# Three stages of a four-layer network kernel: the norm ahead of an involution in a hand-written order, a recurrence in runs of 32 tokens, an expert choice in three pieces

## The chip, the cores and the metric

The kernel runs on one core of a Trainium2 chip. The core has five engines that work side by side: TensorE (PE in the profile; PEld is its loading of weights), VectorE (DVE), ScalarE (ACT), GpSimd (POOL) and SyncE (SP), which in this kernel issues most of the DMAs. They meet through semaphores. SBUF is the memory on the core, 128 partitions wide, and PSUM is the memory that TensorE writes its results to, in eight banks of 512 floats for each partition. The metric is device time in microseconds for the whole program. Three runs of the kernel before gave a median of 8871.85 us (8869.74 to 8875.66).

## The reference

A tensor x of 4 batches, 128 channels and 64 by 64 positions passes four layers. Each has a mixer over positions and a feed-forward part over tokens, each behind a norm over the channels and with its input added back. Three of these eight parts are changed. Cut to what matters, they compute:

```python
def _ln_c(v, eps=1e-6):            # _ln_t is the same over the last axis
    m = jnp.mean(v, axis=1, keepdims=True)
    s = jnp.var(v, axis=1, keepdims=True)
    return (v - m) / jnp.sqrt(s + eps)

# layer 0, mixer: involution, 7 x 7 taps, dilation 2, 8 groups
red = jnp.einsum('bchw,oc->bohw', x, w_reduce) + b_reduce[None, :, None, None]   # 128 -> 32 channels
ker = jnp.einsum('bohw,ko->bkhw', red, w_span) + b_span[None, :, None, None]
...
out = jnp.einsum('bgckhw,bgkhw->bgchw', patches, ker)

# layer 0, feed-forward: a recurrence over the 4096 tokens of a batch
Wx = (flat - mean) * jax.lax.rsqrt(var + BN_EPS) * gamma + beta      # flat = x @ W.T, over all tokens
def step(yt, wx_t):
    yt = jax.nn.sigmoid(wx_t + yt @ Vt)
    return (yt, yt)

# layer 3, feed-forward: two of eight experts for each token
router_probs = jax.nn.softmax(x @ router_w + router_b, axis=-1)
top_p, top_i = jax.lax.top_k(router_probs, K)
top_p = top_p / jnp.sum(top_p, axis=-1, keepdims=True)
...
return jnp.einsum('bnk,bnkc->bnc', top_p, gathered)
```

## The kernel before

The activations stay in SBUF for the whole program, in a tile `xs` of 128 channels by 4 batches by 4096 tokens. Eight phases work on it one after another. A norm over channels is done with TensorE. A matmul with `cent` (the identity less 1/128) takes the mean off 512 tokens, a chunk. ScalarE squares the result, and matmuls with `ewin`, four of them in the four 32-column groups of the array, sum the squares of four chunks into rows of one bank. From that bank come one square root and one reciprocal. A matmul with `ident` then spreads a row of reciprocals over the partitions, and VectorE multiplies. The helper `centred` (L62) does this in two halves, with the square root between them.

A planner orders the instructions, engine by engine, by readiness and position in the program. Inside a block `tc.manual_schedule(engines=ORDERED)` the order of TensorE, ScalarE, VectorE and GpSimd is the order of the code; SyncE's isn't in `ORDERED`.

**Front of the involution (L228 to L279).** For each batch the centred half of the next batch and the scaling half of this one are issued, and the planner weaves them. The normed chunks land in the middle of padded row tiles, 76 wide, of which there are 16: eight for each of two batches in turn. L263 writes each row tile to `inv_image` in DRAM (304 KB). L268 reduces a chunk to 32 channels, repeated four times over the 128 partitions; L276 adds the bias, and L277 writes 256 KB to `inv_reds`. `load` (L211) reads back what a band of 16 rows needs, 16 shifted DMAs of 266 KB and one of 512 KB, all on SyncE's queue. The loads of the first two bands stand behind batches 2 and 3.

**Band loop (L337 to L361).** The pool of its tiles opens at L285. It takes the memory of the front's tiles, so L285 waits for their last use. Sixteen bands follow; band n+2 is loaded when band n is done, since the loaded tiles have two buffers.

**Recurrence (L364 on).** The norm of all 32 chunks (L382) is written to `xn`, laid out like `xs`. 32 matmuls with W and 32 `bn_stats` (L389, L390) give the statistics over all tokens, and these are folded into `wt` and `shift`. Then the 4096 tokens of a batch are cut into 64 runs of 64 tokens, and all runs step together. A first sweep of 20 steps from the run's end gives each run's last state, a second sweep of 64 steps starts each run from its neighbour's. The two pairs of batches, g = 0 and 1, alternate. A step is one matmul by `vt` on top of the inputs (L456) and one sigmoid (L461). The inputs of 4 steps at a time come from one matmul (L439), whose columns are read from `xn` with a step of 64 words. L467 adds the states to `xs`. Between the sweeps is a branch on `flag`, for weights whose row sums are beyond a bound; the branch's body isn't run here.

**Expert choice (L1590 on).** Four chunks make a quad, and a quad's eight halves are the loop of L1734. In a half, `gated` spreads gates over the partitions (L1718) and multiplies (L1724) for the half after it, TensorE multiplies by experts (L1742), and then one piece of `prepare` for the next quad is run by `next(side)`. One of these pieces was all of `choose` (L1637), some thirty small VectorE operations.

Of the kernel before, what the change touches and what calls it, by code (L numbers as in the profile page):

```python
# [17 lines left out]
F32 = mybir.dt.float32  # L18
BF16 = mybir.dt.bfloat16
I32 = mybir.dt.int32  # L20
# [8 lines left out]
P = 128  # L29
# [135 lines left out]


def as_shape(t, like):

    return t.rearrange("p (r w) -> p r w", w=W) if len(like.shape) == 3 else t
# [13 lines left out]
def involution(net):  # L183
# [17 lines left out]
    with ExitStack() as ctx:  # L201
        dram = ctx.enter_context(tc.tile_pool(name="inv_dram", bufs=1, space=bass.MemoryType.DRAM))
        image = dram.tile([B, P, SIDE * SIDE + EXTRA], F32, name="inv_image")
        reds = dram.tile([B, P, N], F32, name="inv_reds")
# [6 lines left out]
        def load(band):  # L211
# [4 lines left out]
            nc.sync.dma_start(red, reds[b, :, r * SPAN : (r + 1) * SPAN])  # L216
# [10 lines left out]
        with tc.tile_pool(name="inv_a", bufs=2) as sb, tc.tile_pool(name="inv_a_ps", bufs=2, space=PSUM) as ps:  # L227
            wred = sb.tile([P, TAPS, CR], F32, name="wred", bufs=1)  # L228
            bred = sb.tile([P, 1], F32, name="bred", bufs=1)
            for k in range(TAPS):  # L230
                nc.sync.dma_start(wred[:, k, :], ins["L0_conv_w_reduce"])
                nc.sync.dma_start(bred[k * CR : (k + 1) * CR], ins["L0_conv_b_reduce"])
            zero = sb.tile([P, PAD * SIDE + EXTRA], F32, name="inv_zero", bufs=1)
            nc.vector.memset(zero, 0.0)
            for b in range(B):
                nc.sync.dma_start(image[b, :, 0 : PAD * SIDE], zero[:, 0 : PAD * SIDE])
                nc.sync.dma_start(image[b, :, (PAD + H) * SIDE : SIDE * SIDE + EXTRA], zero)
            rows = [
                [sb.tile([P, ROWS, SIDE], F32, name=f"inv_rows{i}_{c}", bufs=1) for c in range(NCH)]
                for i in range(2)  # L240
            ]
            for i in range(2):
                for t in rows[i]:
                    nc.gpsimd.memset(t, 0.0)
# [7 lines left out]

            def inside(b, c):
                return rows[b % 2][c][:, :, PAD : PAD + W]

            second = net.centred([0], 1e-6, inside, sb, ps, 4, 2)
            for b in range(B):
                after = net.centred([b + 1], 1e-6, inside, sb, ps, 4, 2) if b + 1 < B else None
                second()
                second = after  # L260
                for c in range(NCH):
                    first = (PAD + c * ROWS) * SIDE
                    nc.sync.dma_start(  # L263
                        image[b, :, first : first + ROWS * SIDE],
                        rows[b % 2][c].rearrange("p r x -> p (r x)"),
                    )
                    pr = ps.tile([P, CH], F32, name="inv_pr", tag="pr")
                    nc.tensor.matmul(  # L268
                        as_shape(pr, inside(b, c)),
                        wred.rearrange("p k r -> p (k r)"),  # L270
                        inside(b, c),
                        start=True,
                        stop=True,
                    )
                    rd = sb.tile([P, CH], F32, name="inv_rd", tag="inv_rd")
                    nc.scalar.activation(rd, pr, AF.Identity, bias=bred)  # L276
                    nc.sync.dma_start(reds[b, :, c * CH : (c + 1) * CH], rd)  # L277
                if b >= B - 2:
                    loaded.append(load(b - (B - 2)))  # L279
# [84 lines left out]
def recurrence(net):  # L364

    tc, nc, ins = net.tc, net.nc, net.ins
    with (
# [13 lines left out]
        xn = sb.tile([P, B, N], F32, name="rnn_xn")  # L381
        net.layernorm(range(B), 1e-5, lambda b, c: xn[:, b, c * CH : (c + 1) * CH], sb, ps, 3)  # L382


        stats = sb.tile([P, B * NCH, nc.vector.BN_STATS_DIM], F32, name="rnn_stats")
        for j in range(B * NCH):
            b, c = divmod(j, NCH)
            pw = ps.tile([P, CH], F32, name="rnn_pw", tag="pd", bufs=3)
            nc.tensor.matmul(pw, wt, xn[:, b, c * CH : (c + 1) * CH], start=True, stop=True)  # L389
            nc.vector.bn_stats(stats[:, j, :], pw)  # L390
# [12 lines left out]
        nc.tensor.transpose(pt[:, 0:P], w, net.ident)  # L403
        nc.vector.tensor_copy(wt, pt[:, 0:P])

# [1429 lines left out]
```

## Time and profile before

The profiled execution took 8533.12 us, of which its span, from the first to the last instruction, is 8531.3 us. It is a single execution, and the median of the three timed runs is 338.7 us above it.

| What | us |
|---|---|
| Median of three runs | 8871.85 |
| Profiled execution | 8533.12 |
| Its span | 8531.3 |
| TensorE busy in the span | 7867.6 |
| VectorE busy | 5591.7 |
| GpSimd busy | 4943.6 |
| ScalarE busy | 3623.6 |

| Stage | from and to, us from the span's start |
|---|---|
| front of the involution, until L285 | 0 to 147.87 |
| bands of the involution | 151.82 to 1221.8 |
| norm and statistics of the recurrence | 1221.8 to 1339.4 |
| first sweep | 1342.4 to 1376.2 |
| second sweep | 1380.1 to 1488.8 |
| expert choice, steady part | 8098 to 8531 |

The page gives busy time by engine, and an engine can be busy in one stage and idle in another, so the stages are read one by one. Where an engine stood idle, the trace names what released it. A wait is put down to the last semaphore that came.

### The profile page before, as it was taken

The numbers are of one execution on the slowest core, as the hardware profiler recorded it, in microseconds if no ns is written. First come the engines' busy times: TensorE is split into PE (matmuls) and PEld (weight loads), VectorE is DVE, ScalarE is ACT, GpSimd is POOL, SyncE is SP. The second block draws the span as 40 slices with busy tenths as digits, with TensorE's granted clock in tenths as the row PEclk, the third lists the DMA queues.
The fourth block names the chain that finished last, engine by engine and source line by source line (L and its number), as shares of the span: only waits on it lengthen the run. The fifth ranks groups of instructions, "written<-read, shape, count | busy, mean of one in ns | idle before, by whom it ended". The sixth has DMA issues, their size and how long they took to land.

```text
span 8531.3 us, 146057 instructions
## 1 busy us (share of the span) xinstructions
PE 7867.6 (92%) x59834; PEld 3483.4 (41%) x59834; DVE 5591.7 (66%) x8297; ACT 3623.6 (42%) x6855; POOL 4943.6 (58%) x2479
## 2 busy tenths in 40 slices
PE   8999998677786688988999999999999999999899
PEld 2333324455555554443444344443444434444233
DVE  5777764688888843226676676776777667677155
ACT  2222222344444441040555555555555555555411
POOL 1444430477777710000888788887888878888600
PEclk8999998899999999997999999999999999999999
DMA  5333310688787723031455455454455544455400
GB/s 182 77 84 71 70 25 4 171 246 237 219 249 208 209 82 131 1 130 40 97 111 110 96 108 108 102 108 106 98 111 107 108 100 105 107 104 110 89 19 21
DMA packets 300201, 951.19 MB, mean 111 GB/s; under 512 B 41925, under 2 KB 114693, under 8 KB 241669
## 3 DMA queue, kind: packets, MB, share of 16 engines
q0 software_dynamic: 142848, 671.18, 33.4%
q1 hardware_dynamic: 156676, 270.60, 10.8%
q8 instruction: 472, 7.73, 0.4%
q14 instruction: 205, 1.67, 0.1%
HBM read 466.83 MB, written 72.17 MB: 63 GB/s over the span
## 4 chain that ended last, share of the span: by engine, by line
PE 55%; DVE 3%; issue 1%; DMA 1%; ACT 1%; POOL 0%; SPq 0%; DVEq 0%; ACTq 0%; POOLq 0%
PE att_pv L1444 15%; PE att_sc L1531 13%; PE att_mx L1388 10%; PE att_sc L1432 5%; PE conv_po L1198 3%; PE top_po L1742 3%; PE top_pw L1718 1%; DVE att_most L1399 1%; DMA moe_w<-in_L_ffn_weight 1%; PE att_sc L1361 0%; PE att_sc L1492 0%; PE att_sc L1475 0%; PE att_mx L1286 0%; PE att_sc L1322 0%; PE moe_acc L995 0%
## 5 line engine op out<-in xcount | busy, mean ns | idle before, releaser
L1463 POOL TENSOR_TENSOR att_acc<-att_acc,att_ex 128x2048 f32<-128x2048 f32 x640 | 2902.1, 4535 | 639.0 <-ACT att_ex L1532 619.7
L1399 DVE TENSOR_REDUCE att_most<-att_mx 128x2 f32<-128x1024 f32 x2016 | 2462.2, 1222 | 1071.7 <-PE att_mx L1388 990.8
L1532 ACT ACTIVATE att_ex<-att_sc 128x512 f32<-128x512 f32 x4096 | 2223.7, 594 | 1772.7 <-PE att_sc L1531 1488.1
L1531 PE MATMUL att_sc<-att_q,att_k 32*128 32x512 f32 x8192 | 2456.6, 606 | 0.0
L1388 PE MATMUL att_mx<-att_k,att_q 32*128 32x512 f32 x8064 | 2293.1, 647 | 12.9 <-DVE att_parts L1411 10.8
L1432 PE MATMUL att_sc<-att_rows,att_ones_b 32*128 32x256 bf16 (+1 forms) x6144 | 1502.6, 306 | 4.8 <-ACT att_ex L1532 4.7
L708 POOL DMA_INDIRECT dcn_g<-dcn_table,dcn_idx x1152 | 1100.0, 955 | 434.9 <-DMA dcn_g<-dcn_table,dcn_idx 119.9
L1444 PE MATMUL att_pv<-att_ex,att_vals 128*32 128x256 f32 x16384 | 1310.3, 391 | 0.0
L319 DVE SCALAR_TENSOR_TENSOR inv_prod<-inv_pk,bspan,inv_seen 128x1024 f32<-128x1024 f32 (+1 forms) x672 | 822.2, 1275 | 228.2 <-PE inv_pk L302 228.2
L1388 PEld LDWEIGHTS att_mx<-att_k,att_q 32*128 32x128 f32 x8064 | 611.1, 185 | 867.5 <-issue 707.2
L317 POOL TENSOR_TENSOR inv_prod<-inv_seen,inv_prod 128x1024 f32<-128x1024 f32 x224 | 528.4, 2359 | 679.1 <-ACT inv_prod L316 533.8
L1444 PEld LDWEIGHTS att_pv<-att_ex,att_vals 128*32 128x32 f32 x16384 | 322.6, 108 | 1319.7 <-issue 1301.5
L749 PE MATMUL dcn_pt<-ident,dcn_sum 128*128 128x128 f32 x2304 | 520.4, 310 | 336.3 <-DVE dcn_sum L733 335.9
L1531 PEld LDWEIGHTS att_sc<-att_q,att_k 32*128 32x128 f32 x8192 | 818.6, 183 | 11.0 <-issue 8.3
L722 ACT ACTIVATE dcn_one<-dcn_g,dcn_w 128x128 f32<-128x128 f32 x1152 | 456.3, 401 | 724.1 <-DMA dcn_g<-dcn_table,dcn_idx 719.2
L302 PE MATMUL inv_pk<-inv_red,wtap 32*96 32x512 f32 (+1 forms) x3584 | 605.7, 637 | 7.8 <-DMA inv_seen<-inv_image 7.8
L316 ACT ACTIVATE inv_prod<-inv_pk,bspan 128x1024 f32<-128x1024 f32 x224 | 249.2, 1113 | 820.9 <-PE inv_pk L302 811.8
L749 PEld LDWEIGHTS dcn_pt<-ident,dcn_sum 128*128 128x128 f32 x2304 | 374.7, 204 | 419.1 <-DVE dcn_sum L733 417.9
L333 PE MATMUL inv_out<-inv_prod,inv_fold 96*32 96x512 f32 (+1 forms) x3584 | 505.8, 606 | 18.3 <-DVE xs L355 18.3
L748 PE MATMUL dcn_pt<-ident,dcn_one 128*128 128x128 f32 x2304 | 477.4, 291 | 18.1 <-ACT dcn_one L722 18.1
L748 PEld LDWEIGHTS dcn_pt<-ident,dcn_one 128*128 128x128 f32 x2304 | 400.0, 205 | 228.3 <-issue 151.2
L725 DVE TENSOR_SCALAR dcn_part<-dcn_g,dcn_w 128x128 f32<-128x128 f32 x1152 | 405.6, 352 | 120.5 <-DMA dcn_g<-dcn_table,dcn_idx 87.7
(329 smaller groups left out, 7419.2 us busy)
## 6 DMA issues: line engine op xcount, KB each, us to landing
att_sum<-att_ex POOLq DMA_DIRECT2D x320, 1024.0 KB, 7.3
inv_seen<-inv_image SPq DMA_DIRECT2D x256, 266.0 KB
moe_w<-in_L_ffn_weight SPq DMA_DIRECT2D x64, 1024.0 KB
dcn_table<-dcn_xt SPq DMA_DIRECT2D x64, 512.0 KB
att_sum<-att_ex SPq DMA_DIRECT2D x32, 1024.0 KB
att_sum<-att_acc POOLq DMA_DIRECT2D x32, 1024.0 KB, 7.1
dcn_g<-dcn_table,dcn_idx POOLq DMA_INDIRECT x1152, 3.7
inv_image<-inv_rows SPq DMA_DIRECT2D x32, 304.0 KB
```

The costliest lines, as they stand in the source:

```text
L302: nc.tensor.matmul(pk[0:m, h, :], wtap[rg, unit, blk, 0:m], red[rg, h * CH : (h + 1) * CH], start=True, stop=True,)
L319: nc.vector.scalar_tensor_tensor(out=of, in0=pk[0:m].rearrange("p h (r x) -> p (h r) x", x=W), scalar=by, in1=view, op0=ALU.add, op1=ALU.mult,
L708: nc.gpsimd.indirect_dma_start(out=g, out_offset=None, in_=rows, in_offset=bass.IndirectOffsetOnAxis(ap=idx[:, j + i, k : k + 1], axis=0),)
L748: nc.tensor.matmul(out, one_, net.ident, start=i == 0, stop=False)
L749: nc.tensor.matmul(out, s, net.ident, start=False, stop=i == 3)
L1388: nc.tensor.matmul(pm[i] if alone else pm[:, i, :], q[r, t * P : (t + 1) * P], ks[r, kc * CH : (kc + 1) * CH], start=True, stop=True,)
L1399: nc.vector.tensor_reduce(most[:, 2 * half : 2 * half + 2, kc], pm, AX.X, ALU.max)
L1432: nc.tensor.matmul(pe[:, cols], ones_b[r], lows[g][r, cols], start=cols.start == 0, stop=False)
L1444: nc.tensor.matmul(block["pv"][r, cols], vals[b][:, t, r], ex[:, h, cols], start=t == 0 and half == 0, stop=t == NT - 1 and half == 1,)
L1463: nc.gpsimd.tensor_add(block["acc"], block["acc"], ex)
L1531: nc.tensor.matmul(pe, ks[r, t * P : (t + 1) * P], qs[c][r], start=False, stop=True)
L1532: nc.scalar.activation(ex[:, h, :], pe, AF.Exp)
```

## The change

There are three edits.

**The front of the involution.** `centred` is replaced by a new helper `normed_groups`, inside a manual order. It goes batch by batch, with the scaling of the batch before woven in after every fourth chunk; variances lag two chunks; the centred chunks go to tiles `ln_d` of their own, copied by ScalarE in batches 1 and 3 and by VectorE in batches 0 and 2. Products then go to 8 row tiles in a ring instead of 16. The reduction to 32 channels is no longer repeated. Four chunks go into the four column groups of one bank, so that there are 8 activations and 8 DMAs to `inv_reds` where there were 32 of each, and `load` reads its part with four DMAs of 32 partitions, one for each repetition. The loads of the first two bands are issued in batch 1.

```diff
+        for p in range(B // n):
+            pv, squares = bank("pv"), []
+            for j in range(PN):
+                stat(p, j, pv, squares)
+                if j % 4 == 1 and j > 4:
+                    variances(j // 4 - 1, pv, squares)
+                if p and j % 4 == 3:
+                    scale(p - 1, j // 4)
+            variances(PN // 4 - 1, pv, squares)
+            rstd = sb.tile([P, CH], F32, name="ln_rstd", tag="ln_rstd", bufs=2)
+            nc.scalar.activation(rstd, pv, AF.Sqrt, bias=self.eps[eps])
+            nc.vector.reciprocal(rstd, rstd)
+            rstds[p] = rstd
+        yield
+        for r in range(PN // 4):
+            scale(B // n - 1, r)
+            yield
...
+        def stat(p, j, pv, squares):
+            pd = bank()
+            nc.tensor.matmul(pd, self.cent, self.chunk(n * p + j // NCH, j % NCH), start=True, stop=True)
+            d = sb.tile([P, CH], F32, name="ln_d", tag="ln_d", bufs=PN + 4)
+            if by_scalar[p]:
+                nc.scalar.copy(d, pd)
+            else:
+                nc.vector.tensor_copy(d, pd)
+            sq = sb.tile([P, CH], F32, name="ln_sq", tag="ln_sq", bufs=6)
+            nc.scalar.activation(sq, pd, AF.Square)
...
-            nc.sync.dma_start(red, reds[b, :, r * SPAN : (r + 1) * SPAN])
+            halves = reds[b, r // 2].rearrange("(q c) t -> c q t", c=CR)[:, 2 * (r % 2) : 2 * (r % 2) + 2]
+            for k in range(TAPS):
+                nc.sync.dma_start(red[k * CR : (k + 1) * CR].rearrange("p (h t) -> p h t", h=2), halves)
...
+            def bank(tag="pd"):
+                return ps.tile([P, CH], F32, name=f"inv_{tag}", tag=tag, bufs={"pd": 2, "pv": 1, "pb": 4, "pr": 1}[tag])
...
+            def reduced(b, g):
+
+                pr = bank("pr")
+                for q in range(4):
+                    _, to = inside(b, 4 * g + q)
+                    part = pr[q * CR : (q + 1) * CR]
+                    nc.tensor.matmul(as_shape(part, to), wred, to, start=True, stop=True)
+                rd = sb.tile([P, CH], F32, name="inv_rd", tag="inv_rd")
+                nc.scalar.activation(rd, pr, AF.Identity, bias=bred)
+                nc.sync.dma_start(reds[b, g], rd)
+
+            def scaled(b, c, d, pb):
+                if c % 4 == 0 and b + c:
+                    reduced(*divmod(2 * b + c // 4 - 1, 2))
+                if b == 1 and c % 4 == 0:
+                    loaded.append(load(c // 4))
+                row, to = inside(b, c)
+                nc.vector.tensor_mul(to, as_shape(d, to), as_shape(pb, to))
...
+            with tc.manual_schedule(engines=ORDERED):
+                for _ in net.normed_groups(1, 1e-6, sb, bank, scaled, (False, True, False, True)):
+                    pass
+                reduced(B - 1, NCH // 4 - 1)
```

**The recurrence.** Runs are 32 tokens long, so there are 128 in a batch, and the second sweep has 32 steps; the first keeps its 20. A step has 256 columns instead of 128, and the inputs of 2 steps make one matmul. `xn` is laid out by token within the run, then batch, then run, so a step's inputs lie side by side, and a normed chunk is written with a step of 512 words. The norm uses the existing helper `normed` in a manual order, one batch's scaling woven into the next batch's statistics; its squares read `xn` where `centred` read PSUM. The product of `vt` with itself and the flag go ahead, and each statistic covers one token place of all runs. `ends` is cleared by GpSimd.

```diff
-        LEN, WARM, MOST, BLK = 64, 20, 1.05, 4
+    LEN, WARM, MOST, BLK = 32, 20, 1.05, 2
...
-        xn = sb.tile([P, B, N], F32, name="rnn_xn")
-        net.layernorm(range(B), 1e-5, lambda b, c: xn[:, b, c * CH : (c + 1) * CH], sb, ps, 3)
+        xn = sb.tile([P, LEN, B, SEGS], F32, name="rnn_xn")
...
+            nc.tensor.matmul(pw, wt, xn[:, t].rearrange("p b s -> p (b s)"), start=True, stop=True)
+            nc.vector.bn_stats(stats[:, t, :], pw)
...
+            parts = [
+                net.normed(
+                    b, 1e-5, lambda c, b=b: xn[:, :, b, c * PART : (c + 1) * PART].rearrange("p t s -> p s t"), sb, bank
+                )
+                for b in range(B)
+            ]
+            for _ in range(NCH + 1):
+                next(parts[0])
...
+            for b in range(1, B):
+                for n in range(NCH):
+                    next(parts[b])
+                    if n % 2:
+                        next(parts[b - 1], None)
+                next(parts[b])
+            for _ in parts[B - 1]:
+                pass
+            for t in range(LEN):
+                statistics(t)
...
-                py, wt, toks[:, t : t + BLK, g * PAIR : (g + 1) * PAIR, :], start=True, stop=True
+                py, wt, xn[:, t : t + BLK, g * PAIR : (g + 1) * PAIR, :], start=True, stop=True
...
-                        if i == g + 1 and t0 + BLK < LEN:
+                        if i == 0 and t0 + BLK < LEN:
                             after[g] = inputs(t0 + BLK, g)
```

**The expert choice.** `choose` yields twice, after the first best and after the exponential of the difference, so that its operations come in three successive halves of the loop; an empty half behind it goes.

```diff
             most0, hit0 = first_best(lg, 0)
+            yield
             rest = small("rest", E)
...
             nc.scalar.activation(share1, share1, AF.Exp)
+            yield
             nc.vector.tensor_scalar_add(share0, share1, 1.0)
...
-            choose(pt, g)
-            yield
+            yield from choose(pt, g)
             yield
```

## The prediction

> **What bounds the kernel now.** I read the page first. Its chain shows a kernel carried by TensorE; most of that is attention, which the edits do not touch.
>
> ```profile
> PE 55%; DVE 3%; issue 1%; DMA 1%; ACT 1%; POOL 0%; SPq 0%; DVEq 0%; ACTq 0%; POOLq 0%
> ```
>
> So only the three edited places count, and each has its own limit. The stage windows (us; busy time and instructions of each engine; granted clock; DMA share; GB/s), and below them two shorter stretches of the front's end:
>
> ```profile
> 10.15:147.87 137.72, 110.95 (x256) 34.38 (x256) 54.98 (x68) 43.72 (x69) 0.00 (x0) 0.88 0.65 223
> 1221.80:1272.90 51.10, 50.99 (x128) 14.19 (x128) 22.44 (x35) 19.11 (x32) 0.00 (x0) 1.00 0.02 4
> 1277.00:1308.90 31.90, 31.09 (x65) 15.40 (x66) 20.12 (x32) 0.00 (x0) 0.00 (x0) 0.50 0.00 1
> 1308.90:1339.40 30.50, 29.73 (x64) 12.66 (x62) 22.38 (x33) 0.00 (x0) 0.00 (x0) 0.92 0.00 0
> 1342.40:1376.20 33.80, 30.38 (x98) 14.95 (x97) 0.85 (x4) 13.01 (x40) 0.00 (x0) 0.92 0.00 0
> 1380.10:1488.80 108.70, 97.81 (x320) 47.22 (x320) 37.58 (x31) 41.86 (x128) 0.00 (x0) 0.98 0.00 1
> ```
>
> ```profile
> 137.00:146.00 9.00, 6.30 (x8) 2.23 (x8) 0.00 (x0) 4.09 (x6) 0.00 (x0) 0.67 0.84 326
> 147.00:163.00 16.00, 11.18 (x44) 2.94 (x48) 9.66 (x10) 2.22 (x2) 4.68 (x2) 0.50 1.02 224
> ```
>
> Row 1 is the involution's front: no engine is full and DMA stands at 0.65. The waits of that stretch name the releaser of the band loop (us, times, longest):
>
> ```profile
> DVE wtap L285 <- DMA inv_reds<-inv_rd: 28.3, 1, 28.3
> ACT inv_rd L276 <- DMA inv_reds<-inv_rd: 18.0, 4, 15.7
> ```
>
> L285 opens the next pool, so it waits until the last row and `inv_rd` write has landed, at 147.87; the bands start at 151.8. Rows 2 to 6 are the recurrence. Its sweep, one block of four steps, in the timeline:
>
> ```profile
> 1390.83 0.75 PE L456 MATMUL rnn_py<-rnn_y,rnn_vt 128*128 128x128 f32 x4 [0.23 <-ACT rnn_y L461]
> 1391.78 0.49 PE L456 MATMUL rnn_py<-rnn_y,rnn_vt 128*128 128x128 f32 x2 [0.20 <-ACT rnn_y L461]
> 1392.11 1.88 PE L439 MATMUL rnn_py<-rnn_xn,rnn_wt 128*128 128x512 f32 x2
> 1392.31 0.37 ACT L461 ACTIVATE rnn_y<-rnn_py,rnn_shift 128x128 f32<-128x128 f32 x1 [0.32 <-PE rnn_py L456]
> 1397.55 0.75 PE L456 MATMUL rnn_py<-rnn_y,rnn_vt 128*128 128x128 f32 x4 [0.23 <-ACT rnn_y L461]
> ```
>
> A block is 6.72 us (1390.83 to 1397.55); an input matmul L439 holds TensorE 1.8 us. In the last stage one wait matters:
>
> ```profile
> PE top_pw L1718 <- DVE top_xg L1724: 21.3, 8, 2.9
> ```
>
> Once per group of four chunks VectorE runs the whole choice in one piece (8185.3 to 8192.1) and TensorE stands 2.9 us for the next products.
>
> [...] each `inv_seen` DMA writes 32 partitions, and row 147 to 163 gives 224 at share 1.02[...]. [...] L439 reads words 256 B apart: median 1035 ns against 592 for the contiguous L389, and L467 (strided in and out) 1296 against about 684[...]. [...] L86 starts only after L84 ends (0.69 then 0.60 us), and the new copy and square will queue likewise.
>
> **Part A, the front.** Removed: 24 of 32 `inv_rd` activations and their 256 KB DMAs, and three quarters of the columns of the reduction; eight row memsets. Added: three more small `red` DMAs per band. Moved: both loads, 20 DMAs each (about 0.45 us of SP's queue apiece, 9 us a load), from behind batches 2 and 3 to batch 1, so past 24 row writes and 6 reds on SP; GpSimd's queue is not touched. Compute: stats come at one chunk per (0.86 matmul + 0.16 + 0.69 copy + 0.60 square + 0.2)/2 banks = 1.27 us, so about 10 us a batch, plus 2 groups of scaling and reduction at about 2 us each: 14 us for batches 1 to 3. From 10.15: 10.4 + 42 + 5.2 (sqrt, 3.35 reciprocal, waits) + 7 for the last rows = about 75. `cent` may also end earlier (it took 8.2 us beside the memsets); that is hidden. DMA: x is in by 24. Then 2 loads x 4.88 MB / 224 GB/s = 43.6; 32 rows x 304 KB at 326/0.84 = 388 GB/s, 25.7; 8 reds 5.4; borders (4 x 459 KB) 4.8. Sum 79.5, so 103.5, and with a little idle at the start and the landing about 110. DMA decides, not compute: rows have only 8 buffers, so batch 2's products wait until batch 1's writes, queued on SP behind the loads, have landed. The second load, formerly hidden under band 0 (to 163), is now ahead of the release. 147.9 to 110: **-38**; from -50 (reads and writes overlap) to -15 (each load leaves the queue empty behind it). The bands keep their 1070 us: their instructions are the same and a load has 67 us per band.
>
> **Part B, norm of the recurrence.** xn becomes [t, b, s], so chunk writes have a 2048 B step. Copies then only write strided: top2's L1668 (64 elements, strided write) takes 217 ns and L1016 (contiguous) 225, so I take 0.69; above, 1.3 as L467. Products read and write strided: 1.3 (L467). The squares read `xn` now, 0.63 to 1.2 on ScalarE, which has room. `rnn_vv` goes first and waits for the `rnn_vt` DMA, issued third at 1221.5: start 1224.2, +2.3. VectorE then: batch 0, 8 x 0.86 + 3 (square, variance, sqrt) + 3.35, to 1238.6, flag work 0.6; three batches of 4 x (2 x 0.69 + 2 x 1.3 + gaps = 4.1) + 0.5 + 3.35, to 1300; last products 8 x 1.35, to 1311; 32 statistics at 0.86 to 0.9, to 1339.5. Before: 1339.4. **0**: the ordering saves what the strides cost. Below -10; above +45 (20 for slow copies, 25 if the interleaved chunks of xn are held to overlap, so that each copy waits for the square before it).
>
> **Part C, sweeps.** 20 + 64 steps of 128 columns become 20 + 32 of 256. The inputs are contiguous: 2 x 0.43 = 0.86 instead of 1.8. Block of two steps on TensorE, in order: step g0 0.43, input 0.86, step g1 0.43, input 0.86, steps 0.43 + 0.43 = 3.43; then g0's sigmoid (0.22 to start, 0.47 by the slope between 365 ns at 128 and 687 at 512, 0.1 back) runs beside g1's last step of 0.43: gap 0.4. Block 3.85. Warm: 1.7 + 10 x 3.85 - 0.85 - 1.2 = 38.2 (33.6 before). Main: 1.7 + 16 x 3.85 - 1.2 = 62.1 (108.7 before). **-42**, less if the wider steps lose their cover (-33), more at -46. VectorE's 32 sums (2.6 a block) fit under 3.85. The branch between (3.9) stays. `shift` is now made after `wt`: two operations of 0.16 us beside 1.7 us of inputs; were that cover gone, 0.3. The memsets of `ends` go to GpSimd, which is idle for 271 us there.
>
> **Part D, the choice.** About 7 us in one piece become 2.6, 2.0 and 2.0 beside 2.5 of products per half; TensorE's half is 5 us. Piece 1 ends 0.5 us before the products are wanted; piece 2 plus the `xs` sum may leave 0.5. The gates come at the seventh step, just before their use in the eighth. 7 x (2.9 - 0.5) = **-17**; from -21 to -8.
>
> **Sum.** -38 + 0 - 42 - 17 = -97 on the span, 8531.3 to 8434. The runs' median 8871.85 is 338.7 above the profiled execution's 8533.12; the waits removed are not matmul throughput, so I subtract the same: 8775.
>
> **Rivals.**
> - *The new layout costs* (0.18): part B at +40, C and the rest as above: -57, 8815. For: L467's and L439's strides. Against: L1668, and ScalarE's room.
> - *The loads come too early* (0.08): A gains 12 only: -71, 8801. For: in-order SP and 8 row buffers. Against: the bytes themselves need only 80 us.
> - *DMA overlaps better* (0.06): A -52, C -46, D -21, B -5: -124, 8748.
> - *The clock takes it back* (0.05): removed idle time lowers the clock in attention (3885 to 8050, 4165 us at 0.99) by 0.02: +83, 8858, no change. For: the unexplained 339 us. Against: attention already runs at 0.99 behind these stages.
> - *Slower* (0.05): the 2048 B step, eight times any stride in this trace's norm or sums, makes each of the 64 copies and products of part B much slower. It decides from 97/64 = 1.5 us extra each; at 2.2 extra, +141 - 97 = +44, 8916.
>
> **Numbers.** Forecast 0.58, own range 8755 to 8800. Faster by over 0.2% (what such a measurement can tell): 0.58 + 0.18 + 0.08 + 0.06 = 0.90; same 0.05; slower 0.05. Range 8735 to 8830: it reaches over the layout case and the good case and leaves out the last two and the tails.
>
> **What would show it.** A right: L285's successor starts near 110 with DMA share near 1 before it; wrong if DMA idles in 40 to 110 or bands lengthen from 1070. B: statistics end near 1339 minus A's gain; a strided copy at 1.3 us or idle VectorE "until ACT ln_sq" would be the layout rival. C: blocks of 3.85 us, last sigmoid about 42 earlier in its stage. D: the wait of L1718's successor falls from 21.3 to under 5. The whole falls if the granted clock in attention moves.

## The result, and the profile after

The changed kernel takes 8778.77 us (median of 4 runs, 8771.40 to 8780.75), the kernel before beside it 8870.80 us (4 runs): ratio 0.9895, 95% interval 0.9877 to 0.9912, so 92 us faster. The forecast was 8775 us, 97 us faster. The sum was nearly right, but two of its four terms were not: one was 13 us too good, another 28 us too small.

The profiles of before and after can't be subtracted as wholes. The deformable phase, which no edit touches, takes 345 us less in the profiled execution of before than in that of after. It goes with the chip used and not with the kernel: experiment 12 below shows the changed kernel with the short phase, and the kernel before takes about 8870 or 8897 us on two of the chips and 8527 or 8530 us on two others. The 338.7 us that the prediction carried over from the profile to the runs are in the main this same difference; to carry them over unchanged was right, though not for the reason given there. Hence the table by stages, all from first and last starts in the traces (us; the starts are rounded to a tenth before they are subtracted). Front: from 0 to the bands' first matmul. Norm: from the bands' last matmul to the start of the statistics' aggregation. Sweeps: from there to the last sigmoid. Choice: from the first to the last expert matmul of the last stage.

| kernel | front | norm | sweeps | choice |
|---|---|---|---|---|
| before | 151.8 | 123.7 | 149.0 | 423.0 |
| changed | 120.3 | 137.2 | 110.7 | 377.9 |
| difference | -31.5 | +13.5 | -38.3 | -45.1 |
| predicted | -38 | 0 | -42 | -17 |

The bands themselves take 1063.9 us before and 1063.3 after. The four differences make -101.4, which lies inside the interval of the measured ratio (78 to 109 us faster); where the 9 us between it and -92 lie was not traced.

The windows of the changed kernel's stages, in the columns of the prediction's window rows (span of the stretch; busy time of TensorE, its weight loads, VectorE, ScalarE, GpSimd; granted clock, that is the share of its full clock that TensorE was given; DMA share; GB/s):

```profile
10.15:116.30 106.15, 64.57 (x255) 18.20 (x253) 44.27 (x52) 35.72 (x61) 0.00 (x0) 0.82 0.90 274
1189.70:1290.50 100.80, 83.74 (x195) 24.36 (x195) 79.84 (x73) 35.93 (x36) 0.00 (x0) 0.83 0.01 2
1290.50:1320.80 30.30, 29.41 (x64) 12.72 (x64) 22.45 (x34) 0.00 (x0) 0.00 (x0) 0.94 0.00 0
1326.00:1364.00 38.00, 35.80 (x113) 20.54 (x111) 0.00 (x0) 18.04 (x39) 0.00 (x0) 0.97 0.00 0
1370.00:1432.80 62.80, 59.30 (x189) 34.63 (x188) 34.75 (x32) 29.66 (x64) 0.73 (x1) 0.98 0.00 0
```

Row 1 is the front: DMA is now nearly full (0.90 instead of 0.65). Row 2 is the norm of the recurrence: VectorE is busy 79.8 of 100.8 us, and TensorE was granted only 0.83 of its clock. The norm before had 1.00 while it took the means off and squared (1221.8 to 1272.9, the second window row of the prediction) and 0.50 while it scaled the chunks (1277 to 1308.9, the third), so a low clock as such is not new there. Row 3 is the statistics, rows 4 and 5 are the two sweeps.

In the changed kernel's timeline (start, duration, instruction) a block of two steps:

```profile
1400.96 1.86 PE L554 MATMUL rnn_py<-rnn_y,rnn_vt 128*128 128x256 f32 x6
1402.66 1.02 PE L537 MATMUL rnn_py<-rnn_xn,rnn_wt 128*128 128x512 f32 x2
1403.52 0.59 PE L554 MATMUL rnn_py<-rnn_y,rnn_vt 128*128 128x256 f32 x2
1403.95 1.02 PE L537 MATMUL rnn_py<-rnn_xn,rnn_wt 128*128 128x512 f32 x2
1404.81 1.03 PE L554 MATMUL rnn_py<-rnn_y,rnn_vt 128*128 128x256 f32 x4
```

From 1400.96 to 1404.81 is 3.85 us, the predicted block, and an input holds TensorE 0.86 us, as predicted. The new program's waits in the front (us, times, longest; the first two of VectorE, the last of SP's queue):

```profile
DVE inv_rows L346 <- DMA inv_image<-inv_rows: 34.7, 4, 21.4
DVE wtap L361 <- DMA inv_reds<-inv_rd: 6.1, 1, 6.1
```

```profile
SPq L338 <- ACT inv_rd L337: 8.8, 2, 6.8
```

L361 succeeds L285. VectorE stands for row buffers whose writes are queued behind the loads; that is the mechanism of part A. The third line was not foreseen: SP's queue stands 6.8 us on a reduction, with the 16 image reads of the first load behind it. DMA during that wait and after it, until the last of the front's writes is issued (the same columns):

```profile
41.00:48.50 7.50, 6.81 (x23) 2.32 (x24) 4.18 (x7) 3.07 (x5) 0.00 (x0) 0.77 0.28 73
48.50:113.20 64.70, 30.70 (x142) 8.20 (x140) 22.29 (x27) 16.25 (x28) 0.00 (x0) 0.76 1.00 276
```

The surprise is the choice. The groups of four chunks in windows, from one set of gate transposes (L1704, now L1804) to the next; two groups of before, then two of the changed kernel:

```profile
8203.05:8257.95 54.90, 51.97 (x170) 20.51 (x169) 28.46 (x61) 8.36 (x14) 0.00 (x0) 0.94 0.05 20
8257.95:8312.70 54.75, 51.81 (x169) 20.58 (x168) 28.43 (x61) 8.36 (x14) 0.00 (x0) 0.94 0.05 20
```

```profile
8484.21:8532.62 48.41, 47.73 (x169) 18.73 (x168) 27.94 (x61) 8.36 (x14) 0.00 (x0) 1.00 0.06 22
8532.62:8581.05 48.43, 47.76 (x170) 18.73 (x168) 27.96 (x61) 8.36 (x14) 0.00 (x0) 1.00 0.06 22
```

The same 169 or so matmul records take 51.9 us of TensorE before and 47.7 after: a group is 6.3 us shorter, not 2.4, and the clock column says why the busy time itself fell. The wait that was to fall from 21.3 us to under 5 is now this one:

```profile
PE top_pw L1818 <- ACT top_gt L1806: 4.7, 7, 0.7
```

The timeline of before around its first stall:

```profile
8131.20 3.60 PE L1742 MATMUL top_po<-top_xg,top_we 128*128 128x512 f32 x8
8137.73 3.86 PE L1718 MATMUL top_pw<-top_gt,ident 32*128 32x512 f32 x8 [2.94 <-DVE top_xg L1724]
8141.52 6.51 PE L1742 MATMUL top_po<-top_xg,top_we 128*128 128x512 f32 x8
8147.87 0.60 PE L1704 MATMUL top_pd<-ident,top_gates 128*128 128x128 f32 x4
8148.40 1.14 PE L1718 MATMUL top_pw<-top_gt,ident 32*128 32x512 f32 x8
```

Four products (eight passes, two for each) take 3.60 us ahead of the 2.94 us stall and 6.51 us behind it (5.4 to 6.0 us behind the six later stalls); the four matmuls of L1718 take 3.86 us instead of 1.14. The granted clock around the fourth stall, which ends at 8303.55, in windows of before:

```profile
8301.00:8304.23 3.23, 0.68 (x3) 0.38 (x3) 3.16 (x11) 0.00 (x0) 0.00 (x0) 1.00 0.15 56
8304.23:8311.05 6.82, 6.82 (x13) 2.99 (x12) 3.59 (x6) 0.00 (x0) 0.00 (x0) 0.50 0.03 12
8311.05:8312.70 1.65, 1.65 (x5) 0.65 (x4) 0.00 (x0) 0.00 (x0) 0.00 (x0) 1.00 0.05 10
```

For 6.83 us the clock is exactly half. A spell of at least this length follows each of the seven stalls.

### The profile page after: what moved, and what is told of

It reads as the page before. It is cut to its first block, busy times and chain, and to the rows that moved or that the text cites. A ratio compares the mean times of both kernels' runs of the same rounds, so it can differ in the third digit from the quotient of the medians.

```text
span 8775.9 us, 145762 instructions
## 1 busy us (share of the span) xinstructions
PE 7837.9 (89%) x59726; PEld 3504.8 (40%) x59726; DVE 5613.8 (64%) x8282; ACT 3540.0 (40%) x6786; POOL 4945.5 (56%) x2473
## 4 chain that ended last, share of the span: by engine, by line
PE 54%; DVE 2%; issue 1%; DMA 1%; ACT 1%; POOL 0%; SPq 0%; DVEq 0%; ACTq 0%; POOLq 0%
PE att_pv L1542 14%; PE att_sc L1629 12%; PE att_mx L1486 10%; PE att_sc L1530 4%; PE conv_po L1296 3%; PE top_po L1842 3%; PE top_pw L1818 1%; DVE att_most L1497 1%; DMA moe_w<-in_L_ffn_weight 1%; PE att_sc L1459 0%; PE att_sc L1573 0%; PE att_sc L1590 0%; PE top_po L1840 0%; PE att_mx L1384 0%; PE att_sc L1420 0%
## 5 line engine op out<-in xcount | busy, mean ns | idle before, releaser
L867 PE MATMUL dcn_out<-dcn_st,dcn_wk 128*128 128x512 f32 x576 | 384.6, 756 | 391.9 <-ACT dcn_st L863 386.1
L863 ACT COPY dcn_st<-dcn_pt 128x512 f32<-128x512 f32 x288 | 167.1, 580 | 1058.8 <-remote 725.1
L846 PEld LDWEIGHTS dcn_pt<-ident,dcn_one 128*128 128x128 f32 x2304 | 440.2, 224 | 266.3 <-issue 194.2
L846 PE MATMUL dcn_pt<-ident,dcn_one 128*128 128x128 f32 x2304 | 515.4, 310 | 28.0 <-ACT dcn_one L820 19.7
L831 DVE SCALAR_TENSOR_TENSOR dcn_sum<-dcn_g,dcn_w,dcn_part 128x128 f32<-128x128 f32 x1152 | 354.0, 345 | 286.8 <-remote 211.7
```

The source lines that it names most:

```text
L846: nc.tensor.matmul(out, one_, net.ident, start=i == 0, stop=False)
```

## The experiments

The theory after seeing the traces: a stall of TensorE is followed by a spell at half clock, and that spell, left out of the prediction, is most of the error in D and part of those in B and C; strided writes are the rest of B. All runs are compared with the kernel before on the same chip; stages in the table at the end of this section.

**1. The choice alone.** The kernel before with part D only:

```diff
         most0, hit0 = first_best(lg, 0)
+        yield
...
         nc.scalar.activation(share1, share1, AF.Exp)
+        yield
...
-        choose(pt, g)
-        yield
+        yield from choose(pt, g)
         yield
```

> The kernel before with part D alone (the choice in three pieces). Theory from the two traces: beside the 2.9 us stall, the matmuls that follow it ran at a granted clock of 0.50 for some 6 us, so a group of four chunks took 55.3 us and will take 48.4: -45 us (7 x 6.5), the last stage 456 -> 411, stage clock 0.94 -> 1.00. The prediction's own term: only the stall goes, -17. Rival: the slow matmuls come from the stages before [...], then -17 here and 55.3 - 2.4 = 52.9 us per group.

Measured: 8829.33 against 8870.04 us, -40.7 (ratio 0.9956, 0.9942 to 0.9970). The stage falls from 423.0 to 378.0, -45.0, with groups of 48.42 us at clock 1.00. The whole effect is the edit's own; nothing of it comes from the stages ahead.

**2. The front alone.** The kernel before with the new involution front and the norm helper it calls (the diff's part A, nothing else).

> The kernel before with part A alone (the involution's front). If the parts are independent: the bands' first matmul at 120 instead of 152, -32 us; the prediction's term -38. A loss or nothing would mean that the front's gain in the changed kernel is paid back by the bands.

Measured: 8834.29 us, -35.8 (0.9960, 0.9946 to 0.9973); first matmul of the bands at 120.8. The gain is kept by the bands. Which of the front's changes makes it (the order, the fewer writes of the reduction, the earlier loads) was not separated, apart from experiments 6 and 7.

**3. The recurrence alone.** The kernel before with the diff's parts B and C.

> The kernel before with parts B and C alone. If independent: norm and statistics +13, scale and sweeps -38, -25 us in all; the prediction's terms 0 and -42 make -42. The untouched deformable phase took 1553 us in the profiled execution of before and 1897 in that of after. If that is a property of the execution and not of the change, its length in these three profiles varies without the run times following the part changed; if the new recurrence lengthens it, this kernel shows 1897 and the two others 1553.

Measured: 8849.61 us, -20.4 (0.9979, 0.9971 to 0.9986). Norm 140.2 (+16.5), sweeps 111.1 (-37.9), together -21.4. The deformable phase is long in the profiles of all three experiments. The three medians add up to -96.9 beside the -92 of the whole: within what these intervals can tell, the parts are independent.

**4. The stall filled.** The kernel before, choice in one piece; idle work keeps TensorE running:

```diff
                 nc.tensor.transpose(pt[:, tok], lt[:, tok], net.ident)
+            px = bank("pd")
+            for _ in range(5):
+                nc.tensor.matmul(px, net.cent, net.chunk(b, r * Q4), start=True, stop=True)
             g = gates[quad % 2]
```

> The kernel before, its choice still in one piece, with five idle-work matmuls of 128x512 (2.96 us at full clock) behind the transposes of each group, so that TensorE doesn't stand while VectorE chooses. Their result is read by nothing. If the half clock after the stall is the hidden cost: clock 1.00, a group 55.3 -> about 51.5, -27 us although 5 matmuls per group are added. If the slow matmuls have another cause (banks, operands, the choice itself): 0, or +20 where the added matmuls run at the slow rate themselves.

Measured: 8854.26 us, -15.8 (0.9980, 0.9971 to 0.9988), stage -19.9. One group in the windows:

```profile
8539.73:8591.73 52.00, 52.00 (x180) 20.52 (x179) 28.40 (x61) 8.36 (x14) 0.00 (x0) 1.00 0.06 21
```

A kernel with five more matmuls per group is faster. TensorE is now busy without a gap, the clock is 1.00, and a group falls from 54.7 to 52.0 although the choice still stands in one piece: 2.7 us are what the half clock costs there. (An added matmul takes 0.88 us and not 0.59, two passes each, so the five are 4.4 us; the expectation of -27 had counted 2.96.) The rival, that the slow products have to do with the choice itself, is out: the choice is unchanged.

**5. The stall half filled.** As 4, with `range(2)`.

> As e4_choice_filled, but two added matmuls (1.78 us at 0.89 each, as e4's profile has them) instead of five: about 1.1 us of the 2.9 us stall remains. e4 without its added work would take 52.0 - 4.46 = 47.6 us per group of four chunks. If a stall of 1.1 us doesn't lower the clock: 47.6 + 1.8 + 1.1 = 50.5 us per group, -34 us against before, clock of the stage 1.00. If any stall lowers it: about 54.4 per group, -6 us, clock 0.94.

Measured: 8882.55 against 8897.42 us (another chip), -14.9 (0.9984, 0.9977 to 0.9991), stage 408.1. Neither number of the expectation came. Windows of two groups, and the timeline behind the stall in the first of them:

```profile
8515.72:8567.71 51.99, 50.76 (x173) 19.95 (x172) 28.31 (x61) 8.35 (x14) 0.00 (x0) 1.00 0.06 20
8567.71:8621.40 53.69, 52.46 (x173) 20.54 (x172) 28.30 (x61) 8.36 (x14) 0.00 (x0) 0.97 0.05 20
```

```profile
8561.33 2.91 PE L1721 MATMUL top_pw<-top_gt,ident 32*128 32x512 f32 x8 [1.23 <-DVE top_xg L1727]
8564.18 3.70 PE L1745 MATMUL top_po<-top_xg,top_we 128*128 128x512 f32 x8
```

Four of the six whole groups show a 1.23 us stall and no loss of clock. In the other two the clock is half for some 3.4 us (an estimate: the eight passes of L1745 take 5.40 us at 8616.17 instead of 3.70), and the group is 1.7 us longer, just half of that. The length of a stall doesn't decide by itself: in the band loop of the changed kernel TensorE stands as long fifteen times in its sixteen bands and keeps its clock (the wait, then the window of the bands):

```profile
PE inv_out L409 <- DVE xs L431: 18.3, 15, 1.2
121.00:1183.00 1062.00, 1043.70 (x7138) 319.97 (x7132) 835.37 (x685) 249.23 (x224) 526.32 (x223) 1.00 0.29 65
```

One thing may set the stalls of experiment 5 apart. In the traces of before and of the changed kernel all changes of the clock lie whole multiples of 3.41 us apart. A grid of that spacing can be laid so that the three stalls here that were followed by half clock (they end at 8507.64, ahead of the first whole group, 8613.32 and 8771.00) reach over a mark of it, and the four others (8561.33, 8667.01, 8719.01 and 8824.64) lie between two marks. Where the grid lies was fitted to these seven stalls, so this is a hint and not shown; and in the bands four of the fifteen stalls reach over a mark of their own trace's grid and cost nothing, so it is no rule for other places. The groups of 52.0 us, as long as those of experiment 4 with three matmuls fewer, show what had been overlooked in the expectation: with the choice in one piece, VectorE is the path there. Behind the stall the eight passes of L1721 take 2.91 us at full clock, because each pair of them needs a bank, and VectorE frees one every 0.6 us (eight products in 4.87 us from 8560.59). That is the third part of what a stall costs here.

**6. The second load late.** The changed kernel with:

```diff
-                if b == 1 and c % 4 == 0:
-                    loaded.append(load(c // 4))
+                if b == 1 and c == 0:
+                    loaded.append(load(0))
...
                 reduced(B - 1, NCH // 4 - 1)
+            loaded.append(load(1))
```

> The changed kernel with the second band's load behind the last inv_rd write instead of in the middle of batch 1. If DMA work ahead of the release sets the front (the prediction's reason): 21.8 us of reads leave the path, VectorE's waits for row buffers (34.7 us in all) mostly go, and the front becomes bound by its computing; bands' first matmul at 100 to 105 instead of 120.25, -15 to -20 against the changed kernel (8759 to 8764), bands unchanged since band 0 takes 67 us. Rival: the front is set by the order of computing and the row buffers alone: 0 to -5. Rival: band 1 or 2 now waits for its load: the gain is paid back in the bands.

Measured: 8788.30 against 8897.42 us (0.9878, 0.9863 to 0.9893), that is -109 where the changed kernel has -92. Bands from 104.0, 16.3 earlier, and as long as ever (1064.0). Its front in the windows, and VectorE's wait for row buffers:

```profile
10.15:100.10 89.95, 66.28 (x255) 18.41 (x253) 44.28 (x53) 35.71 (x61) 0.00 (x0) 0.86 0.86 279
```

```profile
DVE inv_rows L346 <- DMA inv_image<-inv_rows: 12.3, 1, 12.3
```

The waits for row buffers fall from 34.7 to 12.3 us. DMA work queued ahead of the release does set the front.

**7. The loads ahead of the reductions.** The changed kernel with the two conditions at the head of `scaled` exchanged, so that `load` is issued before `reduced`.

> The changed kernel with each load issued before the reduction it stood behind, so that SP's queue doesn't stand 6.8 us (41.2 to 48.1) on an inv_rd before the first load's 16 reads. If the late start is the term that made the front 6 us later than predicted: bands' first matmul 6 to 7 earlier, at 113 to 114 (predicted 110 + 3.9 = 114), -6 us. Rival: the wait only moves to the row writes behind the loads, since the row buffers come free no earlier: 0 to -2.

Measured: 8797.86 us (0.9889, 0.9874 to 0.9904), bands from 115.2, 5.1 earlier. L361 starts at 111.3; the prediction had about 110.

```profile
10.15:111.30 101.15, 65.03 (x255) 17.92 (x253) 44.41 (x52) 35.69 (x61) 0.00 (x0) 0.82 0.95 288
```

The DMA share goes from 0.90 to 0.95: 5.0 of the 6.3 us that L361 was late by are this one wait of SP's queue.

**8. xn by rows.** The changed kernel with the old layout of `xn` under the new order and the new run length:

```diff
-        xn = sb.tile([P, LEN, B, SEGS], F32, name="rnn_xn")
+        xn = sb.tile([P, B, N], F32, name="rnn_xn")
+        toks = xn.rearrange("p b (s t) -> p t b s", t=LEN)
...
-                py, wt, xn[:, t : t + BLK, g * PAIR : (g + 1) * PAIR, :], start=True, stop=True
+                py, wt, toks[:, t : t + BLK, g * PAIR : (g + 1) * PAIR, :], start=True, stop=True
```

(The norm writes `xn[:, b, c * CH : (c + 1) * CH]`, the statistics read the same chunks.)

> The changed kernel with xn stored by batches and chunks as before (norm contiguous), runs of 32 tokens, order by hand and sweeps kept; the sweep's input matmuls then read words 128 B apart. If strided access makes part B's +13: copies 1022 -> 690 ns, products 1196 -> 684, 32 of each, so norm and statistics 131.0 -> 104 to 110; if the handshake through one bank or the four reciprocals make it: over 120. The sweeps pay: input matmuls 1.8 instead of 0.86, block 3.85 -> 5.7, 26 blocks, +48. In all +20 to +28 against the changed kernel.

Measured: 8829.54 us (0.9927, 0.9914 to 0.9941), 28 slower than the changed kernel by the ratios. Norm 124.2 (-13.0), sweeps 151.1 (+40.4), block 5.56. VectorE's groups in the norm (busy, mean ns | idle before), first of the changed kernel, then of this one:

```profile
L162 DVE TENSOR_TENSOR rnn_xn<-rnn_xn,rnn_pd 128x512 f32<-128x512 f32 x32 | 36.6, 1196 | 5.1 <-PE rnn_pd L158 5.0
L142 DVE COPY rnn_xn<-rnn_pd 128x512 f32<-128x512 f32 x32 | 30.7, 1022 | 7.5 <-PE rnn_pd L140 7.5
```

```profile
L142 DVE COPY rnn_xn<-rnn_pd 128x512 f32<-128x512 f32 x32 | 21.6, 684 | 11.7 <-PE rnn_pd L140 11.5
L162 DVE TENSOR_TENSOR rnn_xn<-rnn_xn,rnn_pd 128x512 f32<-128x512 f32 x32 | 20.7, 684 | 14.0 <-PE rnn_pd L158 14.0
```

The 2048 B step costs a copy 338 ns and a product 512 ns. Without it VectorE has 25 us less to do and the norm gains 13; the idle time in the last column shows the rest going into waits for TensorE. In the expectation's own measure that is 118 us for 131.0, between its two answers. (ScalarE's squares get shorter as well, 629 ns for 1078; but no wait of VectorE for a square is on the list of either run, and ScalarE waits 52.7 us for VectorE's copies in the changed kernel.) In the sweeps the input matmuls go from a mean of 634 to 1029 ns. The new layout costs 13 us and brings 40.

**9. Copies into contiguous tiles.** The changed kernel; only the product writes `xn`:

```diff
+        def staged(b, c):
+            if (b, c) in held:
+                return held.pop((b, c))
+            held[b, c] = sb.tile([P, CH], F32, name="rnn_d", tag="rnn_d", bufs=12)
+            return held[b, c]
...
-            nc.vector.tensor_mul(d, d, as_shape(pb, d))
+            to = d if into is None else into(c)
+            nc.vector.tensor_mul(to, as_shape(d, to) if into else d, as_shape(pb, to))
```

> The changed kernel, its recurrence norm copying into contiguous tiles (twelve of 128x512), with only the product writing into the strided xn. If the strided write sets part B's extra: copies 1022 -> 690 ns, products 1196 -> 0.9 to 1.0 (one strided operand instead of two), norm and statistics 131.0 -> 112 to 118, -13 to -19 us; sweeps unchanged at 112. Rival: the product stays at 1196 since its strided write alone sets it: -10. Rival: the handshake over three shared banks holds the pairs at their length: 0 to -4.

Measured: 8423.13 against 8527.25 us (0.9878, 0.9861 to 0.9894), -104. Norm 125.4, -11.8; sweeps 112.1.

```profile
L163 DVE TENSOR_TENSOR rnn_xn<-rnn_d,rnn_pd 128x512 f32<-128x512 f32 x32 | 30.7, 1034 | 9.9 <-PE rnn_pd L158 9.6
L142 DVE COPY rnn_d<-rnn_pd 128x512 f32<-128x512 f32 x32 | 20.9, 677 | 7.6 <-PE rnn_pd L140 7.6
```

A product that only writes with the step takes 1034 ns, about as long as a copy that does (1022); reading with it too adds some 160. The gain lies just below the -13 to -19 of the expectation, near the -10 of its first rival, whose reason (a product still at 1196 ns) did not come.

**10. TensorE kept running beside the reciprocals.** The changed kernel with:

```diff
+        def busy(n):
+            px = ps.tile([P, BLK, PAIR, SEGS], F32, name="rnn_py0", tag="py0", bufs=2)
+            for _ in range(n):
+                nc.tensor.matmul(px, net.cent, net.chunk(0, 0), start=True, stop=True)
...
+                    if n == 1:
+                        busy(3)
                     if n % 2:
                         next(parts[b - 1], None)
...
+            busy(5)
             for _ in parts[B - 1]:
                 pass
```

> The changed kernel with three idle-work matmuls (2.67 us) on TensorE beside each of the first three reciprocals of the recurrence's norm and five beside the last, their result read by nothing. After each 2.3 us stall there the clock falls (0.77 to 0.87 in the windows). If TensorE's slow spell is on VectorE's path: clock about 1.00 in the norm, about 1.5 us per batch and 1.7 at the first statistics, -6 to -8 us. If VectorE, which is busy 85% there, sets the time by itself: 0 to -2, or +2 where the added work stands in front of a needed matmul.

Measured: 8427.94 us (0.9879, 0.9863 to 0.9896), -99. Norm 131.1, -6.1.

```profile
1190.00:1284.40 94.40, 89.19 (x225) 28.04 (x226) 78.12 (x72) 35.63 (x36) 0.00 (x0) 0.94 0.01 2
```

The clock rises from 0.83 to 0.94, and VectorE's waits for L140 and L158 fall from 12.5 to 6.7 us. TensorE's slow spells were on VectorE's path.

**11 and 12. The three improvements together, and the changed kernel again beside them.** Edits 6, 9 and 10 in one kernel; and the changed kernel itself.

> The changed kernel with the second load late (e6), the norm staged in contiguous tiles (e9) and the added idle work beside the reciprocals (e10). If the three are independent, by their stages: -16.3, -11.8 and -6.1, or -34 us against the changed kernel and about -126 against before; less, -28 to -30, if the staged norm has already taken part of what the added work saves. Bands' first matmul at 104, statistics' end 119 to 121 us after the bands' last matmul (137.2 in the changed kernel).

> The changed kernel itself beside e11 on the same chip and in the same rounds: -88 to -100 against before whatever the chip's time for the untouched deformable phase (1850 us from the last sigmoid to the next phase's first sum in the profile of before and in those of e9 and e10, 2190 to 2220 in e1 to e8). If the change itself lengthened that phase, it would be long here on every chip.

Measured on one chip: before 8529.76, changed 8434.80 (0.9886, 0.9871 to 0.9901; -95), the three together 8395.87 us (0.9840, 0.9826 to 0.9853; -134). By stages front -16.9, norm -15.9, sweeps +1.5 against experiment 12: -31 where -34 had been added up; the rest of the 39 us between the medians was not traced. The deformable phase is short here in both (1853 us from last sigmoid to the next phase's first sum): the change has no part in its length.

| kernel | front | norm | sweeps | choice |
|---|---|---|---|---|
| 1 choice alone | 152.4 | 123.0 | 148.9 | 378.0 |
| 2 front alone | 120.8 | 123.2 | 148.9 | 420.7 |
| 3 recurrence alone | 152.8 | 140.2 | 111.1 | 421.4 |
| 4 stall filled | 154.3 | 123.8 | 149.3 | 403.1 |
| 5 half filled | 152.9 | 122.3 | 148.7 | 408.1 |
| 6 second load late | 104.0 | 138.6 | 111.1 | 377.9 |
| 7 loads first | 115.2 | 137.3 | 110.9 | 378.1 |
| 8 xn by rows | 121.9 | 124.2 | 151.1 | 377.9 |
| 9 staged norm | 119.1 | 125.4 | 112.1 | 378.2 |
| 10 reciprocals filled | 119.6 | 131.1 | 112.2 | 378.1 |
| 11 three together | 102.4 | 119.7 | 112.2 | 378.0 |
| 12 changed again | 119.3 | 135.6 | 110.7 | 378.0 |

## Why the prediction was right, and where it wasn't

**Part A: right in mechanism, 6 us off in size.** DMA decides, as forecast: its share is 1.00 from 48.5 to 113.2 us, and with the second load moved out of the way (6) the front shortens by 16.3 us at once. The mis-sized term is "a little idle at the start and the landing", 6.5 us. SP's queue alone stood 6.8 us on the reduction ahead of the first load; experiment 7 takes that away and L361 starts at 111.3, against 110. The working had counted that a load is queued behind the reductions, but not that this queue would wait for one.

**Part B: wrong, +13.5 for 0.** Two steps failed. The first is the copy: "so I take 0.69", from two copies of 64 elements, one strided and one plain, that cost the same. At 512 elements the copy takes 1022 ns. Why the small pair didn't show it stays open: 338 ns over 512 elements would be some 42 ns over 64 (an estimate), more than its 217 against 225 ns leave room for. But its two copies also differ in what they read, and the strided one writes with a step of 128 B and not 2048. With products at 1196 (1300 taken), copies and products make 71.0 us instead of 63.7, +7.3. The upper bound of 1.3 us was on record with L467 as its source, an operation of the same size that reads with a step as well; the copy came out between the two. The second is the sentence of the pairs, 4.1 us each with gaps of 0.2: it took TensorE at full speed behind each reciprocal. Filling those stalls (10) gives back 6.1 us. The two overlap and can't be added up to the 13.5: taking the step out altogether (8) gives 13.0 by itself. (There is also a slip in the working: its terms for the first batch end at 1237.4, and it writes 1238.6.) Writes paid for the step as reads did: 338 ns more for a copy that writes with it (1022 against 684), 350 ns more for a product that only writes with it (1034 against 684), 449 ns more for a square that reads with it (1078 against 629).

**Part C: right; -38.3 for -42.** The block is 3.85 us as worked out, and experiment 8 prices the contiguous inputs at 40 us. What is missing is the start of each sweep, put at 1.7 us for the first inputs. The changed kernel's timeline at the main sweep:

```profile
1366.90 3.78 PE L537 MATMUL rnn_py<-rnn_xn,rnn_wt 128*128 128x512 f32 x4 [3.77 <-issue]
1370.48 1.06 PE L554 MATMUL rnn_py<-rnn_ends,rnn_vt 128*128 128x256 f32 x2
```

Behind the branch's stall of 3.8 us four passes take 3.78 us instead of the 1.7 of the working, at a granted clock of 0.50 (from 1366.90 to 1370.48); with what follows, the main sweep takes 65.1 us (1366.90 to 1431.97) and not 62.1, the warm one 40.1 (1323.60 to 1363.71) and not 38.2. In the warm one ScalarE's table load also waits for `shift` now (1323.88, 1.28 us), where before it ran ahead (1340.8, the first sigmoid at 1344.6); this was seen in the trace and not tried by itself.

**Part D: right in sign, -45.1 for -17.** The step that failed is "7 x (2.9 - 0.5)": it priced the stall at its length. Per group a stall of 2.9 us cost three things. TensorE stands 2.9 us. Then it is held to VectorE's pace while the four banks are filled again, 2.85 us for 1.07 at full clock (5). And it runs at half clock for 6.83 us, which can take 3.4 us; part of this lies under the refilling, and experiment 4 measures 2.7. That is about 7.4 us, of which the changed kernel keeps 0.7 us for `top_gt` and 0.5 us of refilling: 6.2, where the groups show 6.3. What brings such a spell on is not shown. The spells are 6.83 us long behind six stalls of before, 10.24 us at its first, and some 3.4 us behind the two of experiment 5's whole groups. The length of the stall doesn't decide by itself: 2.9 us of idling took the clock in every group of before, and 1.23 us took it in two of six groups of experiment 5, while the stalls of 1.2 us in the bands left it alone. Nor does being busy always give the clock back: in the third window row of the prediction TensorE is busy for 31.09 of 31.90 us at 0.50, with matmuls that read 32 rows (L107, 64 passes of 1136 ns); whether the 32 rows are the reason was not tried. So a stall as short as 1.23 us can count too. The column that showed it was at hand, since the prediction read granted clocks for the recurrence but not for the last stage.

**The rivals.** "The new layout costs" was right about the layout and wrong about its price (+13.5 for +40). "The loads come too early" is shown in small by experiment 6: the second one costs 16 us where it stands, in a front that gains all the same. "DMA overlaps better" and "Slower" did not come: the front shortened by 31.5 and not by 52 us, and a strided copy or product cost 0.34 to 0.51 us more and not 2.2. "The clock takes it back" had the sign wrong: in the choice less idling gave clock back, and attention's clock, on which the whole was to fall, is 0.99 before (3885 to 8050) and after (4176 to 8341). That the sum still came within 5 us of the median is an offset of errors, +6.5, +13.5 and +3.7 against -28, and of 9 us that no stage shows; it is luck and no merit of the working.

## What to carry to other kernels

Price a stall of TensorE at its length, plus the refilling of the buffers behind it, plus up to half of any spell at half clock that follows it (here 2.94 us of standing still, 1.8 us of refilling, 6.83 us at half clock). Not every stall has such a spell (none of the fifteen of 1.2 us in the bands); the granted clock in a window of just that stage shows it, and filling the stall with idle matmuls tests it in one run. Move a stride away from the operand that is read most often (here that brought 40 us in the sweeps and cost 13 in the norm), but price what the other side pays from an instruction of the same size (338 ns at 512 elements, where the pair of 64 elements differed by 8). Before a pool's release, keep only the transfers that its successor needs: a load that was hidden before can come ahead of the release when it is issued earlier (16.3 us here), and one that stands behind a computed value holds the queue (6.8 us here).

## What was not expected of the hardware

- Five added matmuls per group of four chunks made the kernel 16 us faster (experiment 4).
- A stall of 1.23 us lowers TensorE's clock in two of six groups and not in the four others of the same program, and fifteen stalls of 1.2 us in the bands never do; what decides, and how short a harmless stall is, stays open.
- Over 512 elements a write with a step of 2048 B costs VectorE 338 ns more in a copy from PSUM and 350 ns more in a product; ScalarE's square went from 629 to 1078 ns when it had to read with that step.
- The untouched deformable phase differs by some 340 us between the chips used (1850 us on some, 2190 to 2220 us on others); the cause stays open. Making the best front (edits 6 and 7 together) was not tried.
